# Two attention blocks on one core: the last image's projection by the two-level product scheme, its residual moved to SBUF behind it

## The chip, the core and the metric

The kernel runs on one core of a Trainium2 chip. Time is the device time of one execution in microseconds (us); the kernel before takes 2768.14 us, the median of 3 runs (2767.19 to 2768.42). All data are float32. The engines are PE (matrix products, its weight loads shown as PEld), DVE (vector), ACT (activations and copies), POOL (GpSimd) and SP (which here only issues transfers). Each engine takes its instructions in their order and waits at the first one whose inputs are not there.

## What is computed

Eight images of 512 channels and 32 x 32 = 1024 tokens go through two attention blocks. The first has 8 heads of 64 channels, the second one head of 512. Cut to what matters:

```python
def _L0_conv_ref(x, gn_weight, gn_bias, w_qkv, b_qkv, w_proj, b_proj):
    h = group_norm(x, gn_weight, gn_bias)
    qkv = jnp.einsum('oc,bct->bot', w_qkv, h.reshape(B, C, T)) + b_qkv[None, :, None]
...
    weight = jnp.einsum('bct,bcs->bts', q * scale, k * scale)
    weight = jax.nn.softmax(weight.astype(jnp.float32), axis=-1).astype(weight.dtype)
    a = jnp.einsum('bts,bcs->bct', weight, v)
    a = a.reshape(B, C, T)
    out = jnp.einsum('oc,bct->bot', w_proj, a) + b_proj[None, :, None]
    return x + out.reshape(B, C, H, W)

def _L1_conv_ref(x, gamma, beta, q_w, q_b, k_w, k_b, v_w, v_b, p_w, p_b):
    xn = group_norm(x, gamma, beta)
...
    attn = jax.nn.softmax(jnp.einsum('bqc,bck->bqk', q, k) * scale, axis=-1)
    out = jnp.einsum('bqk,bkc->bqc', attn, v).transpose(0, 2, 1).reshape(b, c, h, w)
    return x + conv1x1(out, p_w, p_b)
```

The change concerns `w_proj` times `a`, the bias and `x + out` of the first block, for the last image only.

## The kernel before

**Layout.** An image is four tiles of 128 channels by 1024 tokens (`a[0]` to `a[3]`, `x`, `h`). A channel product `W` (512 x 512) times such an image is split into 2 x 2 blocks of 256 channels by 512 tokens, and done with 7 block products instead of 8 (numbered 1 to 7; the list `ORDER` is 1, 5, 2, 6, 7, 3, 4). Sums of blocks of the image are made first (`image_factors`: tiles `t1`, `t2`, `t4`, and `a[0]` and `a[1]` overwritten, L1028), and the 7 results are added up into the four output blocks.

**One level and two.** `by_channel` with `wino` uses the scheme once: a block product is 4 matmuls of 512 columns, 28 in all. Its results are added from PSUM by DVE (`u_p`, `w_p`, `t_p`, L240 and L251, and the function `done` of the caller). `conv2` uses it twice: each of the 7 block products is again 7 products of 128 channels by 256 tokens, 49 matmuls of 256 columns. For these, `inner_factors` makes 4 differences of 128 x 256 for every outer product (L434, a tile `inner1` to `inner7`, 28 operations in all, on POOL unless an engine is given).

**Inside conv2.** `pair` does one or two outer products side by side, with the steps of `inner_steps`: step 1 starts PSUM bank a, and ACT copies it to bank b (L482); step 6 adds into b, step 2 into a, step 5 starts bank c, step 7 adds into b, and 3 and 4 finish c and b. After each step the result is put to SBUF: copied by ACT when the output block has nothing yet (`put`, L472), or added by DVE to what stands there (`add`, L566). So the steps that add once more into a bank (2, 7, 3, 4) wait until the earlier contents have been read. There are two buffers of each bank. Steps 3 and 4 of a pair come out behind the start of the next pair or stage (`tail`). `more` adds one output block to another on POOL (L571). After each step `run_background(1)` lets one queued piece of work out. The `hooks` of a pair, and a step in `order` that is a function, are emitted at their places.

**Order.** Almost everything around the change is pinned to the order in which it is written (`tc.keep_in_program_order`). Weights go through three slots of `wpool`; `uses` lists them in order of use and `load_weight` issues the next one on SP, which waits there until the slot is free.

**Attention of the last image (b = 7).** `attention0` goes over 4 pairs of heads (`hp`) and two halves of the tokens (`tb`); for the last pair the right half comes first, so the last piece is `a[3]`, left half. It is divided by its softmax sums late: `reciprocals` brings the sums through PSUM (8 matmuls, `sums`), takes the reciprocal on DVE (L652), and sends it through DRAM (`all_rows`, L653 and L673) to get it on all partitions as `r`. For this last piece the three transfers are issued on the ACT queue (`direct`). `scaled` holds the multiplication `a <- a, r` (L734), `steps[7]` makes the second half of `t4` out of the result.

**The projection and what surrounds it.** Beneath the attention `plan` spreads DVE's work on the sums `t` and `steps`. Behind the attention come the loads of `x`, all 28 inner differences of image 6's second block (`ih`, tiles `inner_h1`) on POOL, and `projection`: `by_channel`, product order 1, 5, 6, 7, 2 and so on, `hooks` with the late scale at its third place. `residual` adds result, bias and `x` in one DVE instruction from PSUM (L1057), with six more adds in SBUF (L1061, L1063). `layer1_scores` of image 6 is next: its first stage is a `conv2` called `g1_6` (tiles `psa_g`, `psb_g`, `psc_g`, weights `w_m`), and it begins while the projection's last steps are still running. The result of the projection is stored to DRAM (`spill`, L1076), and its statistics are taken in that second block.

Of the kernel before, what the change touches and what calls it, by code (L numbers as in the profile page):

```python
# [12 lines left out]
ALU = mybir.AluOpType  # L13
# [4 lines left out]
ORDER = (1, 5, 2, 6, 7, 3, 4)  # L18
# [11 lines left out]
def two_attention_blocks_kernel(  # L30
# [143 lines left out]
    def main_path(ctx):  # L174
# [158 lines left out]
        uses = [*layer0, *twice["p"]]  # L333
        for b in range(1, B - 1):
            uses += [*twice["m"], *twice["z"], *layer0, *twice["p"]]
        uses += ["p", *twice["m"], *twice["z"]]
        uses += [*twice["m"], *twice["z"]]
        loaded = []

# [112 lines left out]
        def inner_steps(uid, parity, k, mm, add, y, x, extra, after7, final, early=(), defer=None, flush=None, between=(), order=None):  # L452

            ps, tmp = {}, {}

            def bank(n):
                ps[n] = ps_pools["abc".index(n)].tile([P, 2, 2 * P], F32, tag="ps", name=f"ps{n}_{uid}")[:, :k, :]

            def keep_tmp(what, tag):
                tmp[what] = upool.tile([P, 2, 2 * P], F32, tag=f"{tag}{parity}", name=f"{what}_{uid}")[:, :k, :]
                return tmp[what]

            def put(dst, n, at):

                if x is None:  # L470
                    (d,) = dst
                    nc.scalar.copy(d, ps[n])  # L472
                else:
                    add(dst, ps[n], x(*at))

            def step(j):
                if j == 1:
                    bank("a")
                    mm(ps["a"], 1, True)

                    bank("b")
                    nc.scalar.copy(ps["b"], ps["a"])  # L482
                elif j == 6:
                    mm(ps["b"], 6, False)
                    put([keep_tmp("u2", "u")], "b", (0, 1))
                    while flush:
                        flush.pop(0)()
                    extra(0, 1, True, False)
                elif j == 2:
                    mm(ps["a"], 2, False)  # L490
                    put(y(0, 0), "a", (0, 0))
                    extra(0, 0, True, True)
                elif j == 5:
                    bank("c")
                    mm(ps["c"], 5, True)
                    put([keep_tmp("c5", "w")], "c", (1, 1))
                    extra(1, 1, True, False)
                elif j == 7:
                    mm(ps["b"], 7, False)
                    add(y(1, 1), ps["b"], [tmp["c5"]])  # L500
                    extra(1, 1, False, True)
                elif j == 3:
                    mm(ps["c"], 3, False)
                    add(y(0, 1), ps["c"], [tmp["u2"]])
                    extra(0, 1, False, True)
                elif j == 4:
                    mm(ps["b"], 4, False)
                    if defer is None:
                        put(y(1, 0), "b", (1, 0))
                    else:  # L510
                        add(y(1, 0), ps["b"], x(1, 0), (0,))
                        defer.append(lambda: add(y(1, 0), ps["b"], x(1, 0), (1,)))
                    extra(1, 0, True, True)
                run_background(1)

            def run():
                if order is None:
                    step(1)
                    finish()
                    steps = [6, 5, *between, 2, 7] if between else [6, 2, 5, 7]  # L520
                else:
                    three, four, *rest = tail
                    tail.clear()
                    steps = [{-3: three, -4: four}.get(j, j) for j in order] + rest
                for g in early:
                    g()
                for j in steps:
                    j() if callable(j) else step(j)
                for g in after7:
                    g()  # L530
                tail.extend([lambda: step(3), lambda: step(4)])
                tail.extend(final)

            return step, run

        def conv2(n, f, bias, name, hooks=(), after=(), by_tokens=False, alone=False):

# [40 lines left out]
            def pair(s, products, y, x, final, **kw):  # L580
                def written(r, cc):
                    to = blocks(y, r, cc)
                    if s < 3 or bias is None:
                        return to
                    return [(t, 2 * i + r) for t, (i, _) in zip(to, y)]

                w = weights2[s // 2][:, (0, 2, 0, 1)[s] :]

                def mm(ps, j, start):
                    for i, p in enumerate(products):  # L590
                        wt = w[:, i, j - 1, :]
                        if not by_tokens:
                            matmul(ps[:, i, :], wt, f[p][j], start=start and i == 0, stop=True, skip_group_check=True)
                            continue
                        for h in range(2):
                            matmul(
                                ps[:, i, ts(h, P)], f[p][j][:, ts(h, P)], wt,
                                start=start and (i, h) == (0, 0), stop=True, skip_group_check=True,
                            )

                def extra(r, cc, read, done):
                    if products == (7,):
                        if read:
                            more((0, 1), (0, 1), (1, 1), r, cc)
                        if done:
                            more((1, 1), (1, 0), (1, 1), r, cc)

                return inner_steps(
                    f"{name}_{s}", s % 2, len(products), mm, add, written, x and (lambda *at: blocks(x, *at)),
                    extra, hooks[s] if s < len(hooks) else (), final, (), **kw,  # L610
                )

            second = []
            weights2 = [weight_part((n, 0))]
            pair(0, (1, 5), [(1, 0), (1, 1)], None, [])[1]()
            pair(
                1, (2, 6), [(0, 0), (0, 1)], [(1, 0), (1, 0)], [load_weight, lambda: biased_half(0, 0)], defer=second,
# [426 lines left out]
            hooks[0].append(begin)  # L1044
            return hooks, made

        def projection(b, af, xt, hooks=()):

            norm = GroupNorm(1, f"1_{b}", pinned=b > 0)
            stats, rest = [], []  # L1050

            def residual(i, r, c, ps, u):
                oc = 2 * r + i
                xh = xt[oc][:, ts(c, HT)]

                tc.keep_in_program_order(
                    nc.vector.scalar_tensor_tensor(xh, ps, obias[0][:, oc : oc + 1], xh, ALU.add, ALU.add)  # L1057
                )
                if (r, c) == (1, 1):

                    rest.append(lambda: tc.keep_in_program_order(nc.vector.tensor_add(xh, xh, u)))  # L1061
                elif u is not None:
                    nc.vector.tensor_add(xh, xh, u)  # L1063
                stats.append(lambda: norm.half_stats(oc, c, xh))

                if c == 1 - r:
                    stats.append(lambda: norm.end_stats(oc))

            def add_rest():
                for f in rest:  # L1070
                    f()

            def store():
                spills[b] = spool.tile([KC, P, T], F32, tag="spill", name=f"spill_{b}")
                for c in range(KC):
                    nc.sync.dma_start(spills[b][c], xt[c])  # L1076

            by_channel(
                weight("p"), af, f"p_{b}", residual, middle=(5, 6, 7, 2), hooks=[[], [], hooks, [], [add_rest]],
                after=[load_weight, store],  # L1080
            )
            return norm, stats

        def projection2(b, inner, hooks):
# [91 lines left out]
        for b in range(B):  # L1176
# [18 lines left out]
            V = nc.vector  # L1195
            af, steps = image_factors(a, f"a_{b}", here)
            if last:
                plan = {9: t[:2], 11: t[2:4], 13: [*t[4:6], *steps[:2]], 15: [*t[6:], *steps[2:4]]}
            else:
                plan = {  # L1200
                    9: [*t[:2], lambda: ih[0](V)], 11: [*t[2:4], lambda: ih[1](V), lambda: ih[3](V)],
                    13: [lambda: ih[2](V)], 15: t[4:],
                }
# [3 lines left out]

            if last:
                scaled, _ = attention0(b, q, k, v, a, extra)
                for f in steps[4:7]:  # L1210
                    f()
                psum_pools(f"products_{b}", 2)
                xt = [load_x(b, c, "x") for c in range(KC)]
                for f in ih:
                    f()
                norm1, stats = projection(b, af, xt, [*scaled, steps[7]])
                gf, gsteps = layer1_scores(b - 1, inner)
                _, _, mean, affine = norm_hooks(norm1, f"1_{b}")
                h, loads, applies = begun(load_again, norm1, b, "h1")
# [252 lines left out]
```

## Time and profile before

The profile is of one execution.

| | |
|---|---|
| median of 3 runs | 2768.14 us |
| profiled execution, its own time | 2768.3 us |
| its span in the profile | 2765.8 us |
| granted TensorE clock | 0.999 |
| DMA, mean over the span | 120 GB/s |
| last image's projection, first matmul | 2464.79 us after the span's start |
| first matmul of the scores of image 6 | 2508.35 |

The span goes from the first to the last instruction; the execution's own time lies 2.5 us around it. Busy times by engine, the chain that ended last and the stretch of the projection are shown with the prediction. In the rows of groups, `out<-in` are tile names without their numbers, then the form and count, total us and mean ns of one, and idle time before them with the one that ended it. In a timeline a row can hold several equal instructions (x4); the idle time stands in brackets.

### The profile page before, as it was taken

The numbers are of one execution on the slowest core, as the hardware profiler recorded it, in microseconds if no ns is written. First come the engines' busy times: TensorE is split into PE (matmuls) and PEld (weight loads), VectorE is DVE, ScalarE is ACT, GpSimd is POOL, SyncE is SP. The second block draws the span as 40 slices with busy tenths as digits, with TensorE's granted clock in tenths as the row PEclk, the third lists the DMA queues.
The fourth block names the chain that finished last, engine by engine and source line by source line (L and its number), as shares of the span: only waits on it lengthen the run. The fifth ranks groups of instructions, "written<-read, shape, count | busy, mean of one in ns | idle before, by whom it ended". The sixth has DMA issues, their size and how long they took to land.

```text
span 2765.8 us, 36809 instructions
## 1 busy us (share of the span) xinstructions
PE 2753.6 (100%) x13436; PEld 1762.1 (64%) x13436; DVE 2045.6 (74%) x3214; ACT 998.4 (36%) x1307; POOL 1291.4 (47%) x1384
## 2 busy tenths in 40 slices
PE   9999999999999999999999999999999999999999
PEld 5437736776376853868538694486844968348585
DVE  6587777777777777777777867777678776787776
ACT  1253454214632146312453125531255313633130
POOL 2313605745067440774307752176621766146763
PEclk9999999999999999999999999999999999999999
DMA  7827412344113441144401443114521145112302
GB/s 265 253 91 252 181 32 70 138 159 166 40 63 138 170 162 32 63 161 167 150 24 63 177 182 119 32 55 184 196 98 49 58 153 216 59 54 97 142 24 74
DMA packets 126070, 332.60 MB, mean 120 GB/s; under 512 B 19831, under 2 KB 64695, under 8 KB 114362
## 3 DMA queue, kind: packets, MB, share of 16 engines
q1 hardware_dynamic: 125294, 329.75, 33.6%
q8 instruction: 108, 1.77, 0.3%
q14 instruction: 80, 0.66, 0.1%
q10 hardware_dynamic: 588, 0.42, 0.1%
HBM read 258.14 MB, written 71.99 MB: 119 GB/s over the span
## 4 chain that ended last, share of the span: by engine, by line
PE 99%; DVE 1%; DMA 0%; issue 0%; SPq 0%; DVEq 0%
PE sc L60 16%; PE av L60 16%; PE psb_av L60 6%; PE psb L60 5%; PE psa_av L60 4%; PE psc_av L60 4%; PE psc L60 4%; PE psa L60 3%; PE psb_v L60 3%; PE psb_k L60 3%; PE psb_p L60 3%; PE psb_q L60 3%; PE psb_g L60 3%; PE psb_z L60 3%; PE psc_z L60 2%; PE psa_k L60 2%
## 5 line engine op out<-in xcount | busy, mean ns | idle before, releaser
L700 DVE TENSOR_TENSOR sum<-sum,e 128x1024 f32<-128x1024 f32 x384 | 473.9, 1234 | 35.5 <-ACT e L696 0.9
L696 ACT ACTIVATE e<-sc 128x1024 f32<-128x1024 f32 x512 | 476.1, 1053 | 63.1 <-PE sc L60 62.6
L60 PE MATMUL sc<-q,k 64*128 64x512 f32 x2048 | 456.8, 596 | 0.0
L60 PE MATMUL av<-e,v 128*64 128x512 f32 x2048 | 453.4, 595 | 0.0
L60 PEld LDWEIGHTS sc<-q,k 64*128 64x128 f32 x2048 | 190.1, 185 | 245.9 <-ACT e L696 120.9
L60 PEld LDWEIGHTS av<-e,v 128*64 128x64 f32 x2048 | 141.4, 137 | 299.0 <-issue 288.2
L434 POOL TENSOR_TENSOR inner_h<-x 128x256 f32<-128x256 f32 x16 | 14.8, 924 | 415.9 <-DVE x L1028 415.9
L698 DVE TENSOR_TENSOR sum<-e,e 128x1024 f32<-128x1024 f32 x64 | 79.9, 1249 | 103.6 <-ACT e L696 103.6
L719 ACT COPY a<-av 128x512 f32<-128x512 f32 x64 | 37.5, 586 | 320.1 <-PE av L60 280.6
L126 POOL TENSOR_TENSOR rstd<-ve,mhalf 128x4 f32<-128x4 f32 x16 | 18.8, 1177 | 274.0 <-DVE ve L124 274.0
L60 PE MATMUL psb<-inner,inner_h 128*128 128x256 f32 x448 | 115.6, 380 | 0.0
L60 PE MATMUL psa_av<-e,z 128*128 128x512 f32 x256 | 112.5, 592 | 0.0
L482 ACT COPY psb_v<-psa_v 128x512 f32<-128x512 f32 (+1 forms) x28 | 14.5, 517 | 232.5 <-DVE x L845 176.6
L60 PEld LDWEIGHTS psb<-inner,inner_h 128*128 128x128 f32 x448 | 84.5, 190 | 13.6 <-POOL inner L449 2.1
L60 PE MATMUL psb_z<-w_z,inner_h 128*128 128x128 f32 x672 | 87.5, 276 | 0.0
L60 PE MATMUL psb_g<-inner_h,w_m 128*128 128x256 f32 x336 | 84.9, 381 | 0.0
L776 ACT ACTIVATE e<-e 128x1024 f32<-128x1024 f32 x64 | 65.1, 1052 | 46.7 <-DVE e L766 25.6
L60 PEld LDWEIGHTS psb_z<-w_z,inner_h 128*128 128x128 f32 x672 | 81.4, 192 | 0.5
L60 PEld LDWEIGHTS psa_av<-e,z 128*128 128x128 f32 x256 | 47.4, 190 | 53.6 <-issue 51.7
L771 POOL TENSOR_TENSOR e<-e,e 128x512 f32<-128x512 f32 x64 | 79.3, 1271 | 2.0 <-DVE e L766 1.8
L571 POOL TENSOR_TENSOR v<-v,v 128x256 f32<-128x256 f32 x28 | 20.1, 726 | 125.3 <-DVE u_v L566 121.3
L820 POOL TENSOR_TENSOR t<-e,t 128x1024 f32<-128x1024 f32 x32 | 78.4, 2482 | 0.0
(443 smaller groups left out, 6138.0 us busy)
## 6 DMA issues: line engine op xcount, KB each, us to landing
r<-all_rows SPq DMA_DIRECT2D x78, 256.0 KB
x<-in_x SPq DMA_DIRECT2D x36, 512.0 KB
h<-in_x SPq DMA_DIRECT2D x32, 512.0 KB
spill<-x SPq DMA_DIRECT2D x32, 512.0 KB
x<-spill SPq DMA_DIRECT2D x32, 512.0 KB
out<-x SPq DMA_DIRECT2D x63, 256.0 KB
kept<-a SPq DMA_DIRECT2D x28, 512.0 KB
again<-kept SPq DMA_DIRECT2D x28, 512.0 KB
```

Source lines behind the costliest of these rows:

```text
L60: tc.keep_in_program_order(nc.tensor.matmul(*args, **kw))
L126: nc.gpsimd.tensor_tensor(rstd, ve, mhalf, ALU.pow)
L434: pin(engine.tensor_tensor(dst, x, y, ALU.subtract))
L482: nc.scalar.copy(ps["b"], ps["a"])
L571: nc.gpsimd.tensor_tensor(d, x, y, ALU.add)
L696: nc.scalar.activation(e, sc, AF.Exp, scale=(C // 8) ** -0.5)
L698: nc.vector.tensor_add(total, es[0], e)
L700: nc.vector.tensor_add(total, total, e)
L719: nc.scalar.copy(dst, av)
L771: nc.gpsimd.tensor_tensor(blocks(dst, r, cc)[0], blocks(x, r, cc)[0], blocks(y, r, cc)[0], ALU.add)
L776: nc.scalar.activation(e[c, cc, r], e[c, cc, r], AF.Exp, scale=scale)
L820: on = lambda *a: lambda: tc.keep_in_program_order(nc.gpsimd.tensor_tensor(*a))
```

## The change

The last image's projection no longer uses `by_channel` but `conv2`, with a new order of the outer products: (1, 5), then (7, 3) begun and (6,) within it, then the rest of (7, 3), and (2, 4) at the end. Of these only 2 and 4 take `a[3]`'s left half in their sums. `late` is a list that is emitted between two steps of the pair (7, 3): the scale of `a[3]`, `steps[7]`, the inner differences of product 2 (`ia[2]`, POOL) and 4 (`ia[6]`, DVE), and all but the first piece of image 6's `ih` (24 operations on POOL). The inner differences of `a` for products 1, 5, 7 and 4 are made on DVE, those for 6, 3 and 2 on POOL. `put` can now write two output blocks, with one copy of 256 for each. Under `late`, `more` adds four halves after each of product 6's and (7, 3)'s results: 8 operations on POOL.

`projection` takes the bias and `x` in afterwards: `residual` is a DVE instruction on 128 x 512 with `y` and `x` both in SBUF, eight of them, put into the background list, so that they come out one after each step of the next stage; `store` follows them. `x` is loaded at the pair (7, 3)'s hook. The weights `w_p` come as two pieces of the two-level form. The rest of the kernel is unchanged.

```diff
-        uses += ["p", *twice["m"], *twice["z"]]
+        uses += [*twice["p"], *twice["m"], *twice["z"]]
...
                 if x is None:
-                    (d,) = dst
-                    nc.scalar.copy(d, ps[n])
+                    for i, d in enumerate(dst):
+                        nc.scalar.copy(d, ps[n] if len(dst) == 1 else ps[n][:, i : i + 1, :])
...
-                w = weights2[s // 2][:, (0, 2, 0, 1)[s] :]
-
                 def mm(ps, j, start):
                     for i, p in enumerate(products):
-                        wt = w[:, i, j - 1, :]
+                        at = ORDER.index(p)
+                        wt = weights2[at // 4][:, at % 4, j - 1, :]
...
                 def extra(r, cc, read, done):
+                    if late and done and products in ((6,), (7, 3)):
+                        more((0, 1) if products == (6,) else (1, 1), (1, 0), (1, 1), r, cc)
...
+            if late:
+                weights2.append(weight_part((n, 1)))
+                pair(0, (1, 5), [(0, 0), (1, 1)], None, [load_weight])[1]()
+                ahead, end = pair(
+                    2, (7, 3), [(1, 0), (0, 1)], [(1, 0), (0, 1)], [], order=(-3, 6, -4, 2, *late, 5, 7),
+                )
+                pair(1, (6,), [(1, 0)], [(0, 0)], [], between=[lambda: ahead(1)])[1]()
+                end()
+                pair(3, (2, 4), [(0, 0), (1, 0)], [(0, 0), (1, 0)], [load_weight, *after])[1]()
+                return out
...
-        def projection(b, af, xt, hooks=()):
+        def projection(b, inner, hooks, late):
...
+            hooks[2].append(lambda: xt.extend(load_x(b, c, "x") for c in range(KC)))
+
+            def residual(oc, c):
+                yh = y[oc][:, ts(c, HT)]
+                nc.vector.scalar_tensor_tensor(yh, yh, obias[0][:, oc : oc + 1], xt[oc][:, ts(c, HT)], ALU.add, ALU.add)
...
+            def rest():
+                background.extend(lambda oc=oc, c=c: residual(oc, c) for c in (1, 0) for oc in range(KC))
+                background.append(store)
+
+            y = conv2("p", inner, None, f"p_{b}", hooks, after=[rest], late=late)
...
             if last:
-                plan = {9: t[:2], 11: t[2:4], 13: [*t[4:6], *steps[:2]], 15: [*t[6:], *steps[2:4]]}
+                inner_a, ia = inner_factors(af, f"a_{b}", tc.keep_in_program_order)
+                plan = {
+                    9: [*t[:2], lambda: ia[0](V)], 11: [*t[2:4], *steps[:2]], 13: [*t[4:6], lambda: ia[1](V)],
+                    15: steps[2:4],
+                }
...
                 scaled, _ = attention0(b, q, k, v, a, extra)
-                for f in steps[4:7]:
+                for f in (ia[3], *steps[4:6], lambda: ia[4](V), ia[5], *t[6:], steps[6], ih[0]):
                     f()
                 psum_pools(f"products_{b}", 2)
-                xt = [load_x(b, c, "x") for c in range(KC)]
-                for f in ih:
-                    f()
-                norm1, stats = projection(b, af, xt, [*scaled, steps[7]])
+                norm1, stats = projection(
+                    b, inner_a, [[] for _ in range(4)], [*scaled, steps[7], ia[2], lambda: ia[6](V), *ih[1:]]
+                )
```

More of the change, by code (lines that the diff above doesn't have):

```diff
@@ L534, in inner_steps, with conv2 @@
             return step, run
-        def conv2(n, f, bias, name, hooks=(), after=(), by_tokens=False, alone=False):
+        def conv2(n, f, bias, name, hooks=(), after=(), by_tokens=False, alone=False, late=()):
             out = channel_tiles(name)
@@ L1045, in factors_ahead @@
             return hooks, made
-        def projection(b, af, xt, hooks=()):
[L1049 to L1070, printed above, removed]
-                    f()
+        def projection(b, inner, hooks, late):
+            norm = GroupNorm(1, f"1_{b}", pinned=True)
+            xt = []
+            hooks[2].append(lambda: xt.extend(load_x(b, c, "x") for c in range(KC)))
+            def residual(oc, c):
+                yh = y[oc][:, ts(c, HT)]
+                nc.vector.scalar_tensor_tensor(yh, yh, obias[0][:, oc : oc + 1], xt[oc][:, ts(c, HT)], ALU.add, ALU.add)
             def store():
@@ L1075, in store @@
                 for c in range(KC):
[L1076 to L1081, printed above, removed]
+                    nc.sync.dma_start(spills[b][c], y[c])
+            def rest():
+                background.extend(lambda oc=oc, c=c: residual(oc, c) for c in (1, 0) for oc in range(KC))
+                background.append(store)
+            y = conv2("p", inner, None, f"p_{b}", hooks, after=[rest], late=late)
+            stats = []
+            for c in range(KC):
+                stats += [lambda c=c, i=i: norm.half_stats(c, i, y[c][:, ts(i, HT)]) for i in range(2)]
+                stats.append(lambda c=c: norm.end_stats(c))
             return norm, stats
@@ L1209, in main_path @@
                 scaled, _ = attention0(b, q, k, v, a, extra)
-                for f in steps[4:7]:
+                for f in (ia[3], *steps[4:6], lambda: ia[4](V), ia[5], *t[6:], steps[6], ih[0]):
                     f()
                 psum_pools(f"products_{b}", 2)
-                xt = [load_x(b, c, "x") for c in range(KC)]
-                for f in ih:
-                    f()
-                norm1, stats = projection(b, af, xt, [*scaled, steps[7]])
+                norm1, stats = projection(
+                    b, inner_a, [[] for _ in range(4)], [*scaled, steps[7], ia[2], lambda: ia[6](V), *ih[1:]]
+                )
                 gf, gsteps = layer1_scores(b - 1, inner)
```

## The prediction

> **What bounds the kernel now.** I read the page first: busy time by engine, then the chain that ended last. The lines below give busy microseconds, share of the span and count, then the chain's shares by engine, and two rows of the costliest groups (us in total, mean ns of one, idle before).
>
> ```profile
> PE 2753.6 (100%) x13436; PEld 1762.1 (64%) x13436; DVE 2045.6 (74%) x3214; ACT 998.4 (36%) x1307; POOL 1291.4 (47%) x1384
> PE 99%; DVE 1%; DMA 0%; issue 0%; SPq 0%; DVEq 0%
> ...
> L571 POOL TENSOR_TENSOR v<-v,v 128x256 f32<-128x256 f32 x28 | 20.1, 726 | 125.3 <-DVE u_v L566 121.3
> ```
>
> PE is the bound everywhere: fewer matmul columns are gain, any PE gap is loss, and a gain beyond the matmuls saved is not there to be had (the waits view sums PE's waits to under 6 us in the whole run). So the question is whether the other engines still keep ahead. Next the timeline of the last image's projection: PE (start us, us, what, count of records).
>
> ```profile
> 2464.22 0.64 PE L60 MATMUL sums<-sum,ones 128*32 128x256 f32 x8
> 2464.79 3.70 PE L60 MATMUL psa_p<-a,w_p 128*128 128x512 f32 x8
> 2468.33 3.60 PE L60 MATMUL psc_p<-t_a,w_p 128*128 128x512 f32 x8
> ...
> 2482.06 0.59 PE L60 MATMUL psa_g<-x,w_m 128*128 128x256 f32 x2
> 2482.49 0.59 PE L60 MATMUL psa_g<-t_h,w_m 128*128 128x256 f32 x2
> ...
> 2508.35 1.03 PE L60 MATMUL psa<-g,x 128*128 128x256 f32 x4
> ```
>
> Eight records of 512 columns are 3.43 us apart, one 256-column matmul (two records) 0.43. PE has no gap from T0 = 2464.79 (the projection's start) to 2508.35, when the scores start: 43.56 us. Then POOL, ACT and DVE in the same window:
>
> ```profile
> 2462.70 1.71 POOL L434 TENSOR_TENSOR inner_h<-x 128x256 f32<-128x256 f32 x1
> ...
> 2466.63 1.17 POOL L434 TENSOR_TENSOR inner_h<-x,inner_h 128x256 f32<-128x256 f32 x1
> ...
> 2474.46 0.72 POOL L434 TENSOR_TENSOR inner_h<-x,inner_h 128x256 f32<-128x256 f32 x1
> ...
> 2488.02 1.18 POOL L434 TENSOR_TENSOR inner_h<-t_h,inner_h 128x256 f32<-128x256 f32 x1
> ```
> ```profile
> 2470.05 1.12 ACTq L653 DMA_DIRECT2D all_rows<-line  x1
> 2471.22 0.58 ACT L251 COPY t_p<-psa_p 128x512 f32<-128x512 f32 x1 [3.77 <-issue]
> 2472.00 1.14 ACTq L673 DMA_DIRECT2D r<-all_rows  x2
> ```
> ```profile
> 2466.01 2.35 DVE L1028 TENSOR_TENSOR t_a<-a,t_a 128x512 f32<-128x512 f32 x2
> 2468.28 1.74 DVE L652 RECIPROCAL line<-sums 128x256 f32<-128x256 f32 x1
> 2469.95 2.16 DVE L1028 TENSOR_TENSOR a<-a,a 128x512 f32<-128x512 f32 x2
> ```
>
> Three things are to be seen. POOL already has 28 operations back to back, 2462.70 to 2489.20, 26.5 us (0.95 mean): it is full for the whole 24 us projection. A DVE subtraction of 512 from SBUF takes about 1.1 us here, and a POOL operation 1.17 instead of 0.72, when they meet. And ACT's second copy stood 3.77 us behind a DMA issue that waited for the reciprocal.
>
> [...]DVE's adds with a PSUM input keep their 0.69 us. [...]here 0.727 (L571, POOL) against 0.42 (L434, DVE) for 128x256. [...]
>
> **The change part by part.** Matmuls: 28 of 512 columns (56 records, 7 x 3.43 = 24.0 us) become 49 of 256 (49 x 0.4316 = 21.15). Gain **2.9 us**, all on the path. The two halves of w_p (1792 and 1344 KB for one block of 1792) are in two of the three weight slots long before T0; what they displace is w_m's second half, below.
>
> ACT: the result of product 1 is written by two copies of 256 (0.36 each) for one of 512 (0.58), and the first product's chain is PE, ACT, PE with nothing between: in another image the psa_g to psb_g step takes 1.0 us (438.79 to 439.79), there covered by 16 `sums` matmuls; here those stand before it. So PE waits **0.84** (0.25 to reach ACT, 0.58 copy) before its third matmul. Then the copy c5 stands behind the three DMA issues of the scale's reciprocal (L653, L673), two of which wait for the row to land, 1.95 us after its issue, and behind two copies of 256; PE needs it for matmul 12, due at T0+5.6. Reciprocal done T0+2.1, issue, landing and second issue to about T0+5.2, then 2 x 0.36 and 0.58: T0+6.5. **About 1.0** (0.7 to 1.3).
>
> DVE ahead of the first results: matmul 14 adds into a bank that two adds (p_7_1, p_7_3, L566) must first have read. In the changed instruction order these stand behind t2_a (2 of 512), the reciprocal, a0_7_0 and a0_7_1 (2), inner7_a (4 of 256, new on DVE), t4_h (2) and t4_a (1). From the last exp-sum's end, T0-0.97: 2 x 0.65 (POOL waits for these), 1.74, 2 x 1.1, 4 x 0.88[...], 2 x 1.13, 0.6 to 1.13, adds 2 x 0.35: T0+11.8. PE is there at 13 x 0.43 + 1.8 = T0+7.4. **4.4**[...]. In the kernel before the same list lay beside PE, which asked for none of it so early.
>
> The `late` list, put into the pair of 7 and 3: scale of a0_7_3, second half of t4_a and inner4_a on DVE, inner2_a on POOL, and after it the 24 remaining inner_h of the other image on POOL. DVE's first: scale 0.6 to 1.15, t4_a 0.6 to 1.15, inner4_a 4 x 0.42 to 0.88, with the c5 adds and then the adds of p_7_3 and p_7_1 queued behind them. PE waits for these before matmuls 34 and 36, 1.7 and 2.1: **3.8** (1 without contention). Product 2 and 4 themselves need a0_7_3 at about T0+26, by when inner2_a is done (T0+24.3): no wait of their own.
>
> POOL: before 28 operations; now 28 inner_h, 12 inner_a (products 6, 3, 2) and 8 adds L571, 48 in all. The adds depend on PE and DVE, so POOL cannot run through: after twelve operations it stands until DVE has written p_7_2 behind matmul 20, T0+15.4, with the stalls above (8.6 + 6.2, and 0.6 for DVE). From there, the last L571 add of p_7_3 is the 31st in its queue. 31 x 0.69 (its pitch alone) is 21.4; some five meetings with DVE at 0.45 more make 23.6: T0+39. An earlier L571 add, behind inner2_a, inner5, inner2 and the first of inner6, holds PE's last matmuls of the projection **0.75**.
>
> Residual: before, the STT took PSUM directly (0.74) and six adds followed; now each sum of 49 products goes to SBUF first, and eight STT with two SBUF inputs (L1066, none such in the trace; nearest L845, 0.751[...]) come in the next stage. DVE executes in order: p_7_3's last add (after POOL's 31st, T0+39), five STTs (5 x 0.75 = 3.8 to 5 x 1.2 = 6), and only then g1_6_3, the add that frees psb_g for the next stage's 15th matmul. That is done at T0+45.5. PE is there at (49 + 14) x 0.4316 + 10.8 = T0+38.0. **7.6** (4 to 12). Two more STTs, for the last x load, hold the next bank **0.7**.
>
> SP: w_m's second half goes into a slot of w_p and so waits for PE's last use of it (the 48th matmul, T0+32.3); the last x load and w_z's first half stand behind it on SP. 1344 KB took 5.3 us before (issue 2501.64); all three, 3650 KB at the 412 GB/s of the x loads, are 9 us, T0+42. PE needs w_m's half 24 matmuls (10.4 us) later at the earliest: hidden, with 1 us over at worst, and more behind the wait at psb_g. The spills go out later too (T0+41 to 50); they are read back only behind the scores and z.
>
> Sum: 0.84 + 1.0 + 4.4 + 3.8 + 0.75 + 7.6 + 0.7 = 19.1 of PE waits, less 2.9: **+16.2 us**. The following scores and z stages hold PE without a gap before and after: nothing of it comes back. Against the profiled execution of 2768.3 us (0.16 over the median of the runs, which is nothing here): 2784.5.
>
> **The rivals.** (1) [...]DVE and POOL at their unshared pace. Then the 4.4 goes, the 3.8 falls to 1, POOL's 31st operation ends at T0+32.4 and g1_6_3 can start at 36.6 (0.42 and five times 0.75) against PE's 30.8: 0.84 + 1.0 + 1 + 0.75 + 5.8 + 0.7 - 2.9 = +7.2, **2775.5**. Against it: the pairs of 1.1 and 1.17 in the windows above. (2) POOL keeps the 0.95 mean of before: 31 x 0.95 = 29.5, six more at the g stage: **2790**. For it: that is the same operation in the same stretch; against it: most DVE adds here read PSUM, and these left POOL at 0.72. (3) The other side: PE keeps its pace and the 2.9 is all that is seen, **2765.4**. One mechanism: the queues run ahead, because the adds on POOL come out before the inner_h behind them matter. It decides at the g stage's 15th matmul, due unstalled at 63 x 0.4316 = T0+27.2: less the five STTs, POOL's last p_7_3 add must be done by T0+23, so 31 operations in the 14 us from T0+9.2, 0.45 apiece. The trace has 0.69 as the least. (4) The change doesn't do what it says (late scale still waited for at product 2): at T0+26 against 24.3 there are 1.7 us; a miss would add that much, inside the range.
>
> **How the numbers follow.** Forecast 0.57 (2780 to 2788), rival 1 0.19, rival 2 0.13, rival 3 0.09, rival 4 0.02. What a measurement can tell from no change is about 0.2%, 5.5 us. Rival 3 lies within it; of rival 1 a sixth would too: same 0.12, slower 0.86, faster 0.02 (PE's gain and all its waits together would hardly reach 5.5). Range 2773 to 2790: rival 1 less 2 us below, rival 2 above.
>
> **What would show it.** Right: PE gaps of 4 to 5 us some 7 us behind T0 with DVE as releaser, and of 7 to 8 us at psb_g with DVE L566 named and L1066 in a block before it; POOL L571 adds of p up to 39 us after T0; the first matmul of the scores near T0+60. Wrong: no gap at psb_g, or L1066 landing behind g's adds; a gap that DMA or ACT ends over 2 us.

## The result, and the profile after

The changed kernel takes 2787.88 us (median of 6 runs, 2787.07 to 2788.77), the kernel before 2768.28 (6 runs): a ratio of 1.0071, 95% interval 1.0058 to 1.0084. It is 19.6 us slower; 2784.5 had been forecast. The page after, with the lines that answer to those of before:

```profile
PE 2760.5 (99%) x13478; PEld 1776.2 (64%) x13478; DVE 2058.4 (74%) x3254; ACT 1001.6 (36%) x1315; POOL 1305.7 (47%) x1404
...
PE 96%; DVE 2%; POOL 1%; issue 0%; DMA 0%; ACT 0%; DVEq 0%; ACTq 0%; POOLq 0%
...
L571 POOL TENSOR_TENSOR v<-v,v 128x256 f32<-128x256 f32 x28 | 20.1, 727 | 125.3 <-DVE u_v L566 121.3
```

PE no longer makes up the whole chain: DVE and POOL have 3% of it, where DVE had 1%. And although PE has fewer columns to multiply, its busy time grew by 6.9 us, which no wait explains. The view by stretches, of the projection's start to the scores, first before and then after (start and end, us; busy time and count of PE, PEld, DVE, ACT, POOL; granted PE clock; DMA share; GB/s):

```profile
2464.80:2508.30 43.50, 43.50 (x150) 27.81 (x147) 34.48 (x52) 7.81 (x14) 29.15 (x35) 1.00 0.38 132
```
```profile
2464.80:2528.50 63.70, 49.85 (x192) 40.73 (x189) 45.91 (x84) 10.91 (x22) 45.53 (x56) 0.84 0.39 143
```

The stretch is 20.2 us longer, and so is the span (2786.0 against 2765.8): everything happens here. PE stands still for 63.70 - 49.85 = 13.9 us, and the mean clock that it was granted is 0.84 of full speed. The waits that PE's view names, in total us, times and longest:

```profile
PE psb_p L60 <- DVE p L566: 5.5, 2, 3.7
PE psb_g L60 <- DVE g L566: 4.9, 1, 4.9
...
PE psc_p L60 <- DVE c_p L566: 1.7, 1, 1.7
PE psc_p L60 <- ACT c_p L472: 1.0, 1, 1.0
PE psb_p L60 <- ACT psb_p L482: 0.7, 1, 0.7
```

These are six waits, 13.8 us, at the places that the order of instructions gave. Behind three of them PE's timeline shows something else (start, us, what, count, in brackets the idle time before):

```profile
2476.75 2.92 PE L60 MATMUL psb_p<-inner_a,w_p 128*128 128x256 f32 x6 [3.72 <-DVE p L566]
...
2489.20 1.13 PE L60 MATMUL psc_p<-a,w_p 128*128 128x256 f32 x4 [1.68 <-DVE c_p L566]
2492.12 3.78 PE L60 MATMUL psb_p<-inner_a,w_p 128*128 128x256 f32 x8 [1.79 <-DVE p L566]
...
2499.25 0.59 PE L60 MATMUL psa_g<-x,w_m 128*128 128x256 f32 x2
...
2512.08 3.78 PE L60 MATMUL psb_g<-inner_h,w_m 128*128 128x256 f32 x8 [4.90 <-DVE g L566]
2515.66 1.06 PE L60 MATMUL psa_g<-x,w_m 128*128 128x256 f32 x2
```

The same eight records of 256 columns take 3.78 us at 2512.08, half the pace of the kernel before:

```profile
2494.97 1.89 PE L60 MATMUL psb_g<-inner_h,w_m 128*128 128x256 f32 x8
```

The view by stretches gives the reason in its clock column. The stretches end where that column changes; ahead of each slow spell stand the 3.41 us before it:

```profile
2470.34:2473.75 3.41, 1.64 (x7) 0.78 (x5) 3.41 (x5) 1.45 (x4) 3.33 (x5) 1.00 0.21 79
2473.75:2480.57 6.82, 3.82 (x9) 3.11 (x10) 4.03 (x9) 0.65 (x2) 2.86 (x3) 0.50 0.28 77
...
2487.40:2490.81 3.41, 1.25 (x5) 0.68 (x4) 3.41 (x6) 0.57 (x1) 3.33 (x4) 1.00 0.00 0
2490.81:2497.64 6.83, 5.52 (x13) 4.44 (x14) 3.43 (x9) 0.00 (x0) 6.67 (x10) 0.50 0.00 0
...
2507.88:2511.29 3.41, 0.00 (x0) 0.00 (x0) 3.41 (x4) 0.00 (x0) 3.33 (x4) 1.00 1.06 409
2511.29:2518.12 6.83, 6.04 (x14) 4.87 (x15) 3.50 (x8) 0.58 (x1) 1.41 (x2) 0.50 0.75 280
2518.12:2528.50 10.38, 10.38 (x49) 9.12 (x49) 7.95 (x20) 3.04 (x5) 5.20 (x8) 1.00 0.51 185
```

Three times PE was given half the clock, for 6.8 us each: from 0.7 us into the wait of 3.72, from 0.5 us into the wait of 1.79 that followed the one of 1.68 closely, and from near the end of the wait of 4.90. All the changes lie whole multiples of 3.41 us apart. What comes ahead of a slow spell is a slot of 3.41 us in which PE worked little (1.64, 1.25 and 0.00 us), whether one wait or two took the rest of it. In this trace no slot with 2.24 us of work or more was followed by a fall; in the one of the late residual below, the clock fell after a slot with 0.87 us and not after one with 1.48. As it fell here after 1.64, these figures give no sharp border.

Against 0.214 us a record of 256 columns (eight of 512 were 3.43 us apart before), 12 records from 2476.75 to 2481.31 lost 2.0 us, 12 from 2492.12 to 2497.40 lost 2.7, 16 from 2512.08 to 2518.61 lost 3.1: **7.8 us**. The account: 13.8 of waits, 1.0 for the ends of the matmuls before them (a record is drawn 0.16 us longer than its pitch), 7.8 of half pace, less the 2.9 saved, is 19.7; from the projection's start to the first matmul of the scores it is 20.1 more than before (2464.85 to 2528.53). The difference of 0.4 stays open.

DVE and POOL around the longest wait:

```profile
2505.71 0.42 DVE L566 TENSOR_TENSOR p<-psb_p,p 128x256 f32<-128x256 f32 x1 [2.66 <-POOL p L571]
2506.05 5.38 DVE L1066 SCALAR_TENSOR_TENSOR p<-p,obias,x 128x512 f32<-128x512 f32 x5
2511.35 0.68 DVE L566 TENSOR_TENSOR g<-psb_g,c_g 128x512 f32<-128x512 f32 x1
```
```profile
2482.51 2.09 POOL L571 TENSOR_TENSOR p<-p 128x256 f32<-128x256 f32 x3 [5.91 <-DVE p L566]
...
2504.95 0.73 POOL L571 TENSOR_TENSOR p<-p 128x256 f32<-128x256 f32 x1
2505.63 0.73 POOL L434 TENSOR_TENSOR inner_h<-x,inner_h 128x256 f32<-128x256 f32 x1
2506.31 1.18 POOL L434 TENSOR_TENSOR inner_h<-x,x 128x256 f32<-128x256 f32 x1
```

POOL's operations up to its last add of `p`, 29 of them, run from 2482.51 to 2505.68; DVE's add waits for the last, and five residual instructions of 1.07 us each come between it and the add that PE waits for. They alternate with POOL, whose own go from 0.73 to 1.18.

### The profile page after: what moved, and what is told of

Its sections match the earlier page's. It is cut to its first block, busy times and chain, and to the rows that moved or that the text cites. A ratio compares the mean times of both kernels' runs of the same rounds, so it can differ in the third digit from the quotient of the medians.

```text
span 2786.0 us, 36974 instructions
## 1 busy us (share of the span) xinstructions
PE 2760.5 (99%) x13478; PEld 1776.2 (64%) x13478; DVE 2058.4 (74%) x3254; ACT 1001.6 (36%) x1315; POOL 1305.7 (47%) x1404
## 4 chain that ended last, share of the span: by engine, by line
PE 96%; DVE 2%; POOL 1%; issue 0%; DMA 0%; ACT 0%; DVEq 0%; ACTq 0%; POOLq 0%
PE sc L60 16%; PE av L60 16%; PE psb_av L60 6%; PE psb L60 5%; PE psc_av L60 4%; PE psa_av L60 4%; PE psc L60 4%; PE psa L60 3%; PE psb_g L60 3%; PE psb_v L60 3%; PE psb_k L60 3%; PE psb_q L60 3%; PE psb_z L60 3%; PE psb_p L60 2%; PE psc_z L60 2%; PE psa_k L60 2%
## 5 line engine op out<-in xcount | busy, mean ns | idle before, releaser
L60 PE MATMUL psb_p<-inner_a,w_p 128*128 128x256 f32 x336 | 87.7, 391 | 6.2 <-DVE p L566 5.5
L571 POOL TENSOR_TENSOR v<-v,v 128x256 f32<-128x256 f32 x28 | 20.1, 727 | 125.3 <-DVE u_v L566 121.3
```

The costliest lines, as they stand in the source:

```text
L60: tc.keep_in_program_order(nc.tensor.matmul(*args, **kw))
L571: nc.gpsimd.tensor_tensor(d, x, y, ALU.add)
```

## The experiments

Each is one edit of the changed kernel. The waits are those of its own trace, and T0 is the projection's first matmul.

**The two causes of the long wait: residual and POOL's queue.** The residual was put out later:

```diff
-            hooks[2].append(lambda: xt.extend(load_x(b, c, "x") for c in range(KC)))
...
             def rest():
+                xt.extend(load_x(b, c, "x") for c in range(KC))
...
-            y = conv2("p", inner, None, f"p_{b}", hooks, after=[rest], late=late)
+            y = conv2("p", inner, None, f"p_{b}", hooks, late=late)
...
-                gf, gsteps = layer1_scores(b - 1, inner)
+                gf, gsteps = layer1_scores(b - 1, inner, [[], [rest], [], []])
```

> The changed kernel, with x loaded and the residual's eight STT put out behind the next stage's second pair instead of at once. Theory (POOL's queue AND the block of five STTs before g's first add hold PE, then PE runs at half clock for 6 us): the wait of 4.9 us at psb_g shrinks to under 2, its half-clock stretch (3.1 us lost) goes or shrinks; the STTs meet POOL later and may hold a later add of g, by up to 5 us. Time 2780 to 2786. Rival (POOL's queue alone sets that wait, the STTs cost nothing): the wait stays over 4 us, time 2787 to 2788.

2786.73 us (ratio to the kernel before 1.0067, 1.0050 to 1.0084), 0.7 above what was expected. The reason for the small gain is in PE's timeline:

```profile
2507.44 1.99 PE L60 MATMUL psb_g<-inner_h,w_m 128*128 128x256 f32 x8 [0.30 <-DVE g L566]
...
2522.86 0.70 PE L60 MATMUL psb_g<-inner_h,w_m 128*128 128x256 f32 x2 [4.48 <-DVE g L566]
```

The 4.9 us at psb_g are 0.3, at full pace behind it (eight records in 1.99 us instead of 3.78); but the residual, now 9 us later, holds another add of the same stage for 4.5 us. The block was moved, not hidden. The clock behind this wait shows the slots again:

```profile
2520.31:2523.73 3.42, 0.87 (x4) 0.79 (x5) 3.42 (x6) 0.00 (x0) 2.38 (x3) 1.00 0.90 365
2523.73:2527.14 3.41, 3.41 (x10) 2.66 (x9) 2.36 (x8) 1.36 (x2) 3.13 (x5) 0.50 0.48 192
```

PE goes on at 2522.86 at full clock and is slowed only 0.9 us later, for one slot. The slot before these two had 1.48 us of work, and no fall came behind it. The kernel without the residual altogether (bias and `x` are then not added):

```diff
-                background.extend(lambda oc=oc, c=c: residual(oc, c) for c in (1, 0) for oc in range(KC))
```

> The changed kernel without the eight STT of the residual: bias and x are not added to the projection. Theory (five of them, 5.4 us, stand on DVE between POOL's last add and g's first add): the wait at psb_g, 4.9 us, goes to under 0.5, and the 3.1 us of half pace behind it with it: 8 us, 2779 to 2781. Rival (POOL alone holds psb_g): over 2785.

2779.83 us (1.0041, 1.0027 to 1.0055), no wait at psb_g and eight records there in 1.89 us, the first wait unchanged (3.68). So the residual costs 8 us where it stands: the wait and the slow matmuls behind it. The other way was to shorten POOL's queue:

```diff
-                    b, inner_a, [[] for _ in range(4)], [*scaled, steps[7], ia[2], lambda: ia[6](V), *ih[1:]]
+                    b, inner_a, [[], [], [], ih[2:4]], [*scaled, steps[7], ia[2], lambda: ia[6](V), ih[1]]
...
-                gf, gsteps = layer1_scores(b - 1, inner)
+                gf, gsteps = layer1_scores(b - 1, inner, [ih[4:5], ih[5:], [], []])
```

> The changed kernel, with five of the seven pieces of image 6's inner differences put out later: two behind the projection's last pair, three in the next stage, so that the projection's own adds on POOL no longer stand behind them. Theory (the 31 operations in POOL's queue set the late wait): last POOL add of p about 30 us after T0 instead of 41, the wait at psb_g from 4.9 to under 2 us, no half-clock stretch there: 2778 to 2781. Rival (the STT block on DVE sets it): wait over 3.5 us, 2785 to 2788.

2781.71 us (1.0048, 1.0031 to 1.0065), 0.7 above the range. POOL's last add of p came 32 us after T0 instead of 41, and the wait at psb_g fell to 1.41, at full pace (eight records in 1.99 us). One edit removes that wait and the other leaves 1.4 us of it: it takes POOL's late add *and* the residual between it and PE.

**The first wait: DVE's list.**

```diff
-                for f in (ia[3], *steps[4:6], lambda: ia[4](V), ia[5], *t[6:], steps[6], ih[0]):
+                for f in (ia[3], *steps[4:6], ia[4], ia[5], *t[6:], steps[6], ih[0]):
```

> The changed kernel, with the four differences inner7_a made on POOL instead of DVE, so that DVE's list ahead of the first two adds of the projection is four operations shorter (they took 3.45 us there). Theory (that list holds the 14th matmul): the wait of 3.7 us falls to about 1, [...](2.0 us of half pace gone), and POOL's queue starts up to 3 us earlier although it has four operations more: 2783 to 2786. Rival (that wait has another cause[...]): it stays over 3 us and the time over 2787.

2783.79 us (1.0056, 1.0039 to 1.0073). The 3.7 us wait before the 14th matmul is no longer among PE's waits, and with it the half pace there is gone (six records in 1.56 us instead of 2.92); other waits grew or came new (0.98 for `u_p`, and 2.09 for 1.68), and the one at psb_g stayed (4.68). Four subtractions of 128x256, 3.45 us in DVE's list, were the wait.

**ACT's queue.** The three transfers of the last reciprocal were issued by SP instead of ACT:

```diff
-                        r = reciprocals(totals, uid, False, nc.scalar if direct else None)
+                        r = reciprocals(totals, uid, False, nc.sync if direct else None)
```

> The changed kernel, with the three transfers of the last reciprocal issued by SP instead of ACT, so that ACT's copies no longer stand behind them. Theory (that wait is covered by the DVE list behind it): the wait of 1.04 us for ACT goes, and the next one for DVE grows from 3.7 to about 4.8; time within 1 us of 2787.9. Rival (the ACT wait counts by itself): 1 us or more less, 2786.5 or below.

2787.94 us (1.0073, 1.0056 to 1.0090): the same. The wait for ACT is gone, and the next one, for DVE, is 5.03 instead of 3.72. A wait of PE costs nothing by itself where the next one is set by a time that does not depend on it: there DVE's list. Further on more was exchanged: PE lost less in slow spells (6.2 us instead of 7.8) and waited longer at psb_g (6.18 instead of 4.90).

**The clock.**

```diff
                 def mm(ps, j, start):
+                    fill = {("p_7", 0, 4): 8, ("g1_6", 0, 4): 15}.get((name, s, j), 0)
+                    if fill:
+                        idle = acc_tile(f"idle_{s}_{j}_{name}")
+                        for _ in range(fill):
+                            matmul(
+                                idle[:, : 2 * P], weights2[0][:, 0, 0, :], f[1][1], start=True, stop=True,
+                                skip_group_check=True,
+                            )
```

> The changed kernel, with idle matmuls of 256 columns into an unused bank put on PE ahead of the two longest waits: 8 before the projection's 14th matmul, 15 before the one of psb_g that waited 4.9 us. They cover the waits and add no wait. Theory (PE loses its clock by standing idle, and gets it back after 4 to 6 us): matmuls stay at 0.43 us behind both places, the time falls by 2.0 + 3.1 = 5, to 2782 to 2784. Rival (the half pace comes from something else, such as what the waits let through at once): the half pace stays and the time is 2787 or more.

2784.94 us (1.0058, 1.0042 to 1.0075). PE's timeline and the clock behind the two fillings:

```profile
2474.14 3.62 PE L60 MATMUL idle_p<-a,w_p 128*128 128x256 f32 x16
2477.90 1.56 PE L60 MATMUL psb_p<-inner_a,w_p 128*128 128x256 f32 x6
...
2506.41 6.64 PE L60 MATMUL idle_g<-x,w_m 128*128 128x256 f32 x30
2512.88 1.89 PE L60 MATMUL psb_g<-inner_h,w_m 128*128 128x256 f32 x8
```
```profile
2477.90:2482.40 4.50, 4.50 (x21) 3.98 (x22) 2.62 (x7) 1.22 (x3) 0.60 (x1) 1.00 0.01 4
2512.90:2518.00 5.10, 5.10 (x25) 4.51 (x24) 3.22 (x8) 0.70 (x2) 0.00 (x0) 1.00 0.92 371
```

23 matmuls more, and 2.9 us less. Nothing but PE's standing still was taken away, so that is what halves its pace. That the gain is not the 5 us expected is due to the filling itself: DVE's add came at 2510.65, 44.6 us after T0 (46.5 in the changed kernel: 1.9 earlier, as the first stretch at full pace gives), and PE could have gone on at about 2511.3; 15 matmuls held it until 2512.88.

**All together.** The first two pieces of `inner_h` and t4_h went under the attention, inner7_a to POOL, the late scale behind the first pair, and the transfers to SP. Of the other five pieces of `inner_h` two stay at the `late` place and three go behind the last pair. The residual goes with its loads to the next stage's third pair. To the edits of ACT's queue and of the late residual, shown above, this is added:

```diff
+                    9: [*t[:2], lambda: ia[0](V), ih[0]], 11: [*t[2:4], *steps[:2], ih[1]], 13: [*t[4:6], lambda: ia[1](V), *t[6:]], 15: [*steps[2:4]],
...
+                for f in (ia[3], *steps[4:6], ia[4], ia[5], steps[6]):
...
+                    b, inner_a, [[*scaled, steps[7]], [ia[2], lambda: ia[6](V)], [], ih[4:]], [ih[2], ih[3]]
...
+                gf, gsteps = layer1_scores(b - 1, inner, [[], [], [rest], []])
```

> The changed kernel with all its waits attacked at once: image 6's first two pieces of inner differences and t4_h made under the attention, inner7_a on POOL, the late scale behind pair (1, 5) instead of in (7, 3), the reciprocal's transfers on SP, the rest of the inner differences behind the projection's last pair, x loaded and the residual added from the next stage's third pair on. Theory: [...]PE keeps its clock; projection to scores 45 to 47 us (63.7 in the changed kernel, 43.6 before), some 3 us of waits in the scores for the residual, 2772 to 2776: still slower than before, as the waits left (6 to 8 us) exceed the 2.9 us that the matmuls save. Rival (the waits are set by the amount of work and only move): 2780 or more.

2772.00 us (1.0014, 1.0007 to 1.0021). Its waits:

```profile
PE psb L60 <- DVE e L777: 1.8, 1, 1.8
PE psb_p L60 <- DVE u_p L566: 1.4, 1, 1.4
PE sums L60 <- DVE sum L711: 1.2, 1, 1.2
PE psb_p L60 <- ACT psb_p L482: 0.7, 1, 0.7
PE psb_p L60 <- DVE p L566: 0.6, 1, 0.6
PE psb_g L60 <- DVE g L564: 0.3, 1, 0.3
```

The projection to the scores takes 44.4 us (2466.42 to 2510.82), and PE keeps its pace in all of it (four records of 256 columns in 1.03 to 1.13 us, where half pace takes 1.9; mean granted clock of the execution 0.999). What is left is 6 us of waits: 1.2 of them at the attention's end, where DVE now has more to do, and 1.8 in the scores, where the residual and the statistics behind it ended up. DVE's part under the attention was spread once more (the end of the long line, as in the run above and as here):

```diff
-                    13: [*t[4:6], lambda: ia[1](V), *t[6:]], 15: [*steps[2:4]],
+                    12: t[6:], 13: [*t[4:6], ia[1]], 15: [*steps[2:4]],
```

> The kernel with all waits attacked, with DVE's work under the attention spread out further (t4_h one step earlier, inner5_a on POOL), since there the sums of the last block came 1.2 us late. Theory: that wait goes, the projection's own waits fall a little, and the residual's wait in the scores (1.8 us) stays: 1 to 2 us under the 2772.0 of that kernel, 2770 to 2771.5, still not under the kernel before. Rival (POOL's four operations under the attention slow the sums as much): 2772 or more.

2770.56 us (1.0008, 1.0000 to 1.0016; 2770.05 to 2771.28 against 2767.83 to 2769.75). The wait at `sums` is gone. The interval of the ratio reaches down to 1.0000, but each of these runs took longer than each of the kernel before: the change, put right as far as it was tried, gives no gain.

## Why the prediction was right, and where it was off

The sign came from the right step: PE saves 2.9 us of columns, and the other engines' lists behind it cost several times that. That the size came so near, 3.4 us short, is in part luck: a cost of 7.8 us was left out, and the waits were put 4.3 us too long.

- *ACT, 0.84 and 1.0*: measured 0.71 and 1.04, with 0.16 more each for the end of the matmul before. The other waits carry the same 0.16. But the second of them costs nothing by itself, as the run with SP showed: the forecast counted waits one after the other, which is right only as long as the next one is counted from the delayed time, as it was there.
- *DVE's list, 4.4*: measured 3.72 and 0.16. The slowing of DVE and POOL beside each other was in the trace about as the author had estimated it (0.88): inner7_a took 0.83 to 0.94 each on DVE instead of 0.42, beside POOL's 0.78 to 1.17 instead of 0.72. One of each together took 0.87 us, less than the 1.11 of the two alone (0.42 and 0.69). Why they slow each other is not shown. Rival 1 is out, and so is rival 2: POOL's operations up to the last add took 0.80 each, a wait of 0.93 included, not 0.95.
- *The late list, 1.7 and 2.1*: 1.68 and 1.79. Products 2 and 4 did not wait for the scale, so the change does what it says.
- *POOL holding the projection's last matmuls, 0.75, and the second bank, 0.7*: neither occurred. PE came later to both, because it ran slow before; that this is why is not tried, but in the two runs where the slow spell ended sooner after psb_g (inner7 on POOL, transfers on SP) 0.53 us of the second one were there.
- *POOL's 31 operations, 23.6 us*: 23.2, but for 29 operations. The count was two too high, and a wait of 0.93 us for DVE within the row was not in the sum; the two errors nearly cancel. They began at T0+17.7 instead of 15.4 and ended at T0+40.8 instead of 39.
- *Five STTs, up to 1.2 each, and 7.6 us at psb_g*: the 1.2 was the author's estimate; 1.07 each beside POOL (0.71 for the two that POOL left alone), and 4.90. The add was done at about T0+47.2 (45.5 forecast), but PE was there 4 us later than thought.
- *w_m hidden*: no wait for a transfer in the stretch.
- *"The first matmul of the scores near T0+60"*: T0+63.7.
- *ACT's 3.77 us in the kernel before*: 1.1 of them are the recorded issue itself (the row of L653). In the other 2.6 us the profile shows nothing on ACT; the issue was recorded at 2470.05, when the reciprocal had just ended (2470.02).

The step that failed is one that the sum does not have: it took a waiting PE to go on at the pace it had before ("PE is there at (49 + 14) x 0.4316 + 10.8"). It lost 7.8 us at half clock behind its waits. The forecast waits (19.1) were too long by 4.3 against the 14.8 measured with their ends, for the same reason: a PE that runs slow reaches the next late bank later. The two leave the 3.4 us by which the forecast was low, but for 0.1. The run with idle matmuls shows the cause for the first and third of the three slow stretches; that the second pair of waits acts in the same way is read from its clock column, not tried by itself.

In numbers, the three slow spells have a granted clock of 0.50 and last 6.8 us each, twice 3.41; one in the run with the late residual lasts 3.41. PE need not stand still for the whole slot ahead of a spell: it had worked 1.64 and 1.25 us in two of them, so that two waits of 1.7 and 1.8 us did what one of 4.9 did. The kernel before has no wait in this stretch (PE busy for all of the 43.50 us, clock 1.00), so its trace could not show it there.

## What to carry to other kernels

A faster product scheme on a saturated engine pays only if the engines that feed it have room: count the operations in each of their queues between the first result and the last one needed, and look whether what is new stands ahead of an add that frees a bank. Price a wait of the matrix engine at its length, and look at the granted clock behind it: here, where the waits left PE 1.64, 1.25 and 0.00 us of work in a slot of 3.41, the half pace behind them added 2.0, 2.7 and 3.1 us, less what the next wait took back. A deferred piece of work must be put where its engine has slack; here the residual held the next stage at one place, then at another, then the scores, while with the form it replaced, an add straight from PSUM (0.73 to 0.75 us each), PE had no gap in the stretch.

## What was not expected of the hardware

The half pace after waits, above: a matmul of 256 columns went from 0.43 us to between 0.85 and 0.90, in spells of 6.8 us, or 3.41 for one with the late residual. Their starts and ends lie whole multiples of 3.41 us apart in the changed kernel, and the spell need not start when the wait ends: with the late residual PE had gone on at full pace for 0.9 us before it was slowed. And 23 useless matmuls in place of the waits made the kernel 2.9 us faster (2784.94 against 2787.88).
